# A graph-network kernel's setup in program order, with the first block's loads in two parts

## The chip, the cores and the metric

The kernel runs on one core of one Trainium2 chip. The metric is the device time of one execution in microseconds (us), the median of several runs. A core has five engines, each with an instruction queue of its own that is worked off in order: TensorE (PE, matrix products; its weight loads are shown as PEld), VectorE (DVE), ScalarE (ACT), GpSimd (POOL) and SyncE (SP, which here only issues DMAs and loads registers). An engine waits for another one, or for a DMA, on semaphores. A DMA is issued by an instruction of SP, ACT or POOL; it then runs on the core's 16 DMA engines and reports when its data has landed.

## What is computed

The kernel computes one layer of a graph network over 6250 nodes and 206250 edges, a residual sum and a layer norm. Cut to what matters here:

```
msg  = concat([x[dst], edge_attr])            # one row per edge, 64 + 64 wide
h    = relu(msg @ W1a.T + b1a)                # 128 wide
h    = h @ W1b.T + b1b
sums = segment_sum(h, src, 6250)              # rows of edges added at their source node
agg  = sums / max(counts, 1)
z    = relu(concat([x, agg]) @ W2a.T + b2a) @ W2b.T + b2b
x    = layernorm(x + concat([z, x]) @ Wr.T + br)
```

The edges are sorted by `dst`; `src` is in no order. So the gather of `x[dst]` is local, and the sum over `src` is what has to be brought together.

## The kernel before

The edges are cut into 1612 tiles of 128, and 13 tiles make a block: 124 blocks. Since the edges are sorted by `dst`, all the nodes that one block needs lie in a window of 60 nodes (`WIN`) that begins at a number, the window's start, of that block's own. For each block the kernel does the following.

- `group` (lines 1345 to 1370) loads what the block needs, on SP's queue. For the first eight blocks (`NEAR`) these are the target numbers of the block's 1664 edges, repeated over 60 partitions (`rhs<-in_dst_o`, L1352), the edges' features (`rhs<-in_edgeT`, L851), and the 60 node rows of the window (`rt<-in_xT`, L1356). The last load starts at the window's start, so SP first loads that number into a register out of `win_i` (L1355), a small table that DVE makes from the loaded `base_i` (L742).
- `columns` (L1386, DVE) compares the target numbers with the 60 nodes of the window, whose numbers stand in `near_f` (L986). The result is the upper half of the left operand `rhs` of the first layer.
- `window` (L1394, PE, and L1395, ACT) multiplies the window's node rows with the node half of W1a; ACT copies the result into `mv`, the other operand.
- `hidden` (L1427, PE, and L1431, ACT) is the first layer: one matmul of two passes per tile, and a relu by ACT into `orow`, three or four tiles at a time.
- `carried`, `bins_of`, `counts_of` and `slots` give each edge its place in a table of rows in DRAM, sorted by source node: DVE finds the edge's bin, the high bits of `src` (`hi`, L751 and L752, then L1092), and runs a scan over the block's tiles (L1098). PE makes counts of it with two triangular matrices, `less_ones` and `less_before` (L1140, L1141, into `cnt_ps`, of which there is one). DVE reduces them (L1238) and writes the row numbers `rowidx` (L1247).
- `scatter` (L1479, POOL) writes the 13 tiles of `orow` to the table, one indirect DMA per tile. From block 4 to block 109 six or nine tiles of a block are first sorted by PE in groups of four rows (`join`, `marks`, L1280 to L1343), and the scatter of a group (L1451) writes four rows at a time. So these blocks take nine or seven scatters in place of 13.
- Rows that are complete are read back (L1559, SP), and PE adds them up per node with one-hot matrices (L1593 on DVE, L1613 on PE). At the end of the kernel the node layers and the layer norm follow.

The order on PE, ACT, DVE and SP in the loop over the blocks is the order in which the program is written. Before the loop (lines 686 to 1800) a scheduler sets the order. POOL's order is the scheduler's throughout. The loop begins with this prologue, in which the numbers are those of blocks:

```
for g in range(3):
    made[g] = group(g)
window(0)
carried(0)
counts = counts_of(0, *bins_of(0))
columns(0)
slots(0, counts)
```

After it, block 0's `hidden` runs in four parts of 4, 3, 3 and 3 tiles; then come `window(1)`, `columns(1)`, `carried(1)` and `bins_of(1)`, and so on. In what is set up before the loop, `part_f` is each partition's own number, `in_win` (L941) and `from_win` (L939) are made from it, and `ramp` (L937) is the row 0 to 127. `one_w`, `before_w`, `four_w`, `more_w`, `less_w`, `of_quads`, `bases` and `even` are used by the joins from block 4 on; `ones` by the loads of node rows and by ACT from later blocks on; `bad` and `out_of` by checks.

Of the kernel before, what the change touches and what calls it, by code (L numbers as in the profile page):

```python
# [18 lines left out]
P = 128  # L19
# [459 lines left out]
NODES = 8  # L479

# [8 lines left out]
def fast_path(  # L489
# [69 lines left out]
    def direct(k):  # L559
        return BLK - JOIN * joined(k)  # L560
# [124 lines left out]

    base_i = const.tile([1, NGR], I32, name="base_i")
    nc.sync.dma_start(base_i, first.rearrange("(o g) -> o g", o=1))
# [8 lines left out]
    nc.sync.dma_start(src_i[:, :HEAD], srcT[:, :HEAD])  # L696
    near_i = const.tile([P, NEAR], I32, name="near_i")
# [18 lines left out]
    nc.vector.memset(mvs, 0.0)  # L716
# [12 lines left out]
    nc.vector.tensor_scalar(eye_b, diff_i, 0.0, BIG, op0=ALU.is_equal, op1=ALU.mult)  # L729
    ones = const.tile([P, P], F32, name="ones")  # L730
    nc.vector.memset(ones, 1.0)
# [3 lines left out]
    nc.vector.tensor_copy(part_f, part_i)  # L735
    nc.gpsimd.memset(near[: D + 1], 1.0)
    for e, ep_ in enumerate(epochs):
        ep_.tot = const.tile([P, 2 * HALF], F32, name=f"tot{e}")
# [3 lines left out]
    nc.vector.tensor_scalar(win_i, base_i, float(N - WIN), None, op0=ALU.min)  # L742
# [6 lines left out]
    def bins(c0, c1):  # L749
        tmp_i = lent(NT, NT)[:, c0:c1].bitcast(I32)  # L750
        nc.vector.tensor_scalar(tmp_i, src_i[:, c0:c1], 7, None, op0=ALU.arith_shift_right)  # L751
        nc.vector.tensor_copy(hi[:, c0:c1], tmp_i)  # L752
        nc.vector.tensor_scalar(tmp_i, src_i[:, c0:c1], P - 1, None, op0=ALU.bitwise_and)
        nc.scalar.copy(lo[:, c0:c1], tmp_i)

    ident = const.tile([P, P], F32, name="ident")
    make_identity(nc, ident)
    nc.vector.tensor_copy(mvs[:, :, H:], ident[:, None, WIDE : WIDE + 2].to_broadcast([P, MV, 2]))
# [6 lines left out]
    with (  # L765
# [83 lines left out]
        def edges(g):  # L849
            n = direct(g)  # L850
            nc.sync.dma_start(rhss[g % EDGES][:D, : n * P], edgeT[:, ((g + 1) * NG - n) * P : (g + 1) * NG * P])  # L851
# [9 lines left out]
        nc.vector.memset(out_of, 0.0)  # L861
# [77 lines left out]
        nc.vector.tensor_scalar(from_win, part_f, -1.0, float(D), op0=ALU.mult, op1=ALU.add)  # L939
        in_win = steady[:, RAMP : RAMP + 1]  # L940
        nc.vector.tensor_scalar(in_win, part_f, float(-D), None, op0=ALU.add)  # L941
# [5 lines left out]
        def starts_at(joints):  # L947
# [11 lines left out]
        one_w = const.tile([P, P], BF16, name="one_w")  # L959
        nc.vector.memset(one_w, 1.0)  # L960
        before_w = const.tile([P, P], BF16, name="before_w")
        nc.vector.scalar_tensor_tensor(
            before_w, diff_i, 0.0, eye_b, op0=ALU.is_gt, op1=ALU.add
        )
        less_ones = const.tile([P, P], BF16, name="less_ones")
        nc.vector.memset(less_ones, -1.0)
        less_before = const.tile([P, P], BF16, name="less_before")
# [3 lines left out]
        bins(0, HEAD)  # L971
# [12 lines left out]
        for g, i in ((2, NQB * 2), (3, NQB * 4)):  # L984
            assert NQB * (BLK - JOIN * g + 1) + i <= 512 and NQB * JOIN * g + NQB * 3 * (3 - g) <= 512
        nc.vector.tensor_scalar(  # L986
            near_f[D:WIDE, :], near_i[D:WIDE, :], float(N - WIN), in_win[D:WIDE, :], op0=ALU.min, op1=ALU.add
        )

        def row_of(value, name):  # L990


            w = const.tile([P, P], BF16, name=name)
            nc.vector.memset(w, 0.0)
            nc.vector.memset(w[:1, :], value)
            return w

        four_w, more_w, less_w = row_of(float(QUAD), "four_w"), row_of(1.0, "more_w"), row_of(-1.0, "less_w")
# [3 lines left out]
        for c, b in zip(of_quads, bases):  # L1002
            nc.vector.memset(c, FULLQUADS)
            nc.vector.memset(c[:, :, NQB:], FULLQUADS + P)
            nc.vector.memset(b, 0.0)
# [3 lines left out]
        nc.vector.memset(even_1, FULLQUADS)  # L1009
        even = even_1.to_broadcast([P, NQB])  # L1010
# [1180 lines left out]
```

## Time and profile before

| | |
|---|---|
| median of three runs | 1558.59 us |
| the three runs | 1558.59, 1557.15 and 5025.22 us |
| the profiled execution | 1557.99 us |
| its span, first to last instruction | 1556.1 us |
| mean granted TensorE clock | 0.978 |

The profile is of one execution. A row of its timeline gives the start and the length in us, the engine (SPq and ACTq are the instructions with which SP and ACT issue a DMA), the line of the program, the operation, what is written from what, the size (partitions x elements) and how many instructions are taken together; in brackets stands the time that the engine was idle before, and what ended it. A table by stages gives, for stretches of the span, how long each engine was busy and how many instructions it ran, the granted clock, the share of time in which the DMA engines were busy, and what they moved per second. Groups of instructions are listed by line with their busy time, the mean of one in ns, and the idle time in front of them.

### The profile page before, as it was taken

How to read it: one execution, taken by the hardware profiler on the slowest of the kernel's cores; microseconds unless marked ns; L12 is line 12 of the kernel's file. 1: busy time of each engine (PE TensorE's matmuls, PEld its weight loads, DVE VectorE, ACT ScalarE, POOL GpSimd, SP SyncE). 2: the span in 40 equal slices, each digit the busy share in tenths (PEclk: the TensorE clock that was granted, in tenths of full speed). 3: DMA queues.
4: the chain of work that ended last, by engine and by line, in shares of the span. 5: the costliest groups of instructions: out<-in, count | busy, mean ns of one | idle time of the engine just before them, and what ended most of it. 6: DMA issues, size and time to landing. Idle time of an engine off the chain costs nothing.

```text
span 1556.1 us, 33587 instructions
## 1 busy us (share of the span) xinstructions
PE 1438.4 (92%) x10958; PEld 1271.3 (82%) x10958; DVE 1334.3 (86%) x2819; ACT 1111.2 (71%) x2393; POOL 1149.6 (74%) x1232
## 2 busy tenths in 40 slices
PE   6689999968999999899999989999999999999996
PEld 5567777757888888788887878889888899999885
DVE  7588988879888988889888989999999887877886
ACT  3289999878888888788878869887877743342014
POOL 5777777777777777777777777777777777777733
PEclk9699999999999999999999999999999999999998
DMA  8877888768887888687777667677687899999883
GB/s 211 232 234 269 284 271 269 254 221 254 268 255 226 266 263 259 195 258 229 228 248 217 219 216 230 218 230 239 207 264 237 254 325 332 347 317 305 276 243 97
DMA packets 248712, 387.82 MB, mean 249 GB/s; under 512 B 43285, under 2 KB 180311, under 8 KB 248527
## 3 DMA queue, kind: packets, MB, share of 16 engines
q1 hardware_dynamic: 167661, 220.81, 49.2%
q0 software_dynamic: 47904, 122.68, 22.2%
q10 hardware_dynamic: 32962, 42.08, 8.0%
q8 instruction: 89, 1.46, 0.4%
q14 instruction: 96, 0.79, 0.2%
HBM read 214.09 MB, written 171.32 MB: 248 GB/s over the span
## 4 chain that ended last, share of the span: by engine, by line
PE 52%; DMA 16%; ACT 13%; DVE 9%; issue 6%; POOL 3%; ACTq 1%; SPq 0%; DVEq 0%; POOLq 0%
PE place L1613 20%; PE place L1325 9%; DMA rows<-orow,rowidx 8%; PE place L1427 8%; PE place L1340 8%; DMA rt<-rows 4%; ACT marks L1291 3%; DMA rows<-orow,qidx 3%; ACT marks L1295 2%; ACT rhs L1381 2%; POOL rows L1479 2%; ACT orow L1431 2%; DVE oh L1593 2%; ACT rj L1330 2%; DVE ramp L1191 1%
## 5 line engine op out<-in xcount | busy, mean ns | idle before, releaser
L1479 POOL DMA_INDIRECT rows<-orow,rowidx x922 | 899.8, 976 | 289.8 <-issue 148.7
L1613 PE MATMUL place<-rt,oh 128*128 128x129 f32 x3952 | 483.9, 277 | 32.3 <-ACT orow L1343 18.2
L1613 PEld LDWEIGHTS place<-rt,oh 128*128 128x128 f32 x3952 | 466.6, 192 | 46.2 <-ACT orow L1343 19.7
L1593 DVE TENSOR_TENSOR oh<-ramp,rt 128x768 f32<-128x768 bf16 (+4 forms) x391 | 309.0, 823 | 35.5 <-DMA rt<-rows 34.2
L1431 ACT ACTIVATE orow<-place 128x512 f32<-128x512 f32 (+1 forms) x266 | 145.0, 545 | 186.5 <-PE place L1427 181.2
L1451 POOL DMA_INDIRECT rows<-orow,qidx x230 | 225.2, 979 | 70.1 <-issue 22.2
L1340 PE MATMUL place<-mv,rj 128*128 128x130 f32 x1840 | 243.1, 282 | 35.6 <-ACT rj L1330 30.2
L1280 DVE TENSOR_TENSOR marks<-quad_ramp,ramp 128x1024 fp32r<-128x1024 f32 x230 | 268.6, 1212 | 5.0 <-ACT z_act L1194 5.0
L1427 PE MATMUL place<-mv,rhs 124*128 124x128 f32 x1844 | 265.2, 289 | 5.5 <-ACT orow L1431 5.5
L1340 PEld LDWEIGHTS place<-mv,rj 128*128 128x128 f32 x1840 | 220.5, 192 | 51.0 <-ACT rj L1330 37.5
L1325 PE MATMUL place<-marks,side 128*128 128x512 f32 x690 | 261.3, 408 | 0.0
L1427 PEld LDWEIGHTS place<-mv,rhs 124*128 124x128 f32 x1844 | 232.8, 198 | 7.2 <-ACT orow L1431 5.7
L1325 PE MATMUL place<-marks,rest 128*64 128x512 f32 x690 | 234.6, 394 | 0.0
L1325 PEld LDWEIGHTS place<-marks,side 128*128 128x128 f32 x690 | 130.9, 190 | 50.2 <-issue 0.8
L1295 ACT ACTIVATE marks<-marks,ones 128x512 fp32r<-128x512 f32 x230 | 166.8, 725 | 4.1
L1291 ACT ACTIVATE marks<-quad_ramp,z_act 128x512 fp32r<-128x512 f32 x230 | 166.0, 722 | 3.4 <-PE place L1325 0.9
L1343 ACT ACTIVATE orow<-place 128x260 f32<-128x260 f32 x460 | 159.3, 390 | 9.8 <-PE place L1340 1.4
L1098 DVE TENSOR_TENSOR_SCAN had<-ramp,bins 128x400 bf16<-128x400 bf16 (+2 forms) x124 | 128.4, 1036 | 23.9 <-ACT orow L1418 11.3
L1330 ACT COPY rj<-place 128x512 f32<-128x512 f32 x230 | 131.2, 571 | 0.8 <-PE place L1325 0.8
L1381 ACT ACTIVATE rhs<-rhs,ones 60x896 f32<-60x896 f32 (+2 forms) x116 | 123.8, 1067 | 3.0
L1379 ACT ACTIVATE rhs<-rhs,from_win 60x896 f32<-60x896 bf16 (+2 forms) x116 | 123.6, 1065 | 2.6
L1325 PEld LDWEIGHTS place<-marks,rest 128*64 128x64 f32 x690 | 93.5, 136 | 37.7 <-issue 0.4
(194 smaller groups left out, 1586.9 us busy)
## 6 DMA issues: line engine op xcount, KB each, us to landing
rt<-rows SPq DMA_DIRECT2D x194, 390.0 KB
rt<-rows SPq DMA_DIRECT2D x97, 325.0 KB
rows<-padrow ACTq DMA_DIRECT2D x24, 1040.0 KB
rhs<-in_edgeT SPq DMA_DIRECT2D x88, 224.0 KB
enat<-in_edgeJ SPq DMA_DIRECT2D x88, 192.0 KB
rows<-orow,rowidx POOLq DMA_INDIRECT x922
rt<-rows SPq DMA_DIRECT2D x40, 260.0 KB
rt<-rows SPq DMA_DIRECT2D x48, 195.0 KB
```

What stands on the lines that cost most here:

```text
L1280: nc.vector.tensor_tensor(m[:, :n, :], all_q[:, None, :].to_broadcast([P, n, QUAD * P]), z[:, :n, None].to_broadcast([P, n, QUAD * P]), op ...
L1291: nc.scalar.activation(m[:, t, :], all_q, AF.Square, bias=z_acts[k][:, i * JOIN + t : i * JOIN + t + 1], scale=-1.0)
L1295: nc.scalar.activation(m[:, t, :], m[:, t, :], AF.Relu, bias=ones[:, :1], scale=-1.0)
L1325: done[k, f"turn{i}"] = nc.tensor.matmul(ps[: w.shape[1], :], w, m[:, t, :], start=t + p == 0, stop=last and p == 1).ins.name
L1330: nc.scalar.copy(rj, ps)
L1340: done[k, f"join{i}"] = nc.tensor.matmul(ps[:, j, :], rj[:, (g0 + j) * P : (g0 + j + 1) * P], m, start=True, stop=True).ins.name
L1427: done[k, c] = nc.tensor.matmul(ps[:, j, :], rhs[:WIDE, of * P : (of + 1) * P], m[:WIDE, :H], start=True, stop=True).ins.name
L1431: nc.scalar.activation(orow_of(k, k0, n)[:, :, :H], ps[:, :n, :], AF.Relu)
L1451: s = nc.gpsimd.indirect_dma_start(out=qep.rows.rearrange("(q r) f -> q (r f)", r=QUAD), out_offset=bass.IndirectOffsetOnAxis(ap=qidx[:, q ...
L1479: s = nc.gpsimd.indirect_dma_start(out=ep_.rows, out_offset=bass.IndirectOffsetOnAxis(ap=rowidx[:, k % RING * BLK + j : k % RING * BLK + j ...
L1593: nc.vector.tensor_tensor(res[:, at_tile : at_tile + nb * n, :], ramp[:, None, :].to_broadcast([P, nb * n, P]), node[:, :, None].to_broadc ...
L1613: m = nc.tensor.matmul(of_bin(b), oh[:, at, :], rows, start=i == 0, stop=i == len(of) - 1)
```

## The change

The change touches what runs before the loop and in block 0.

- The setup on PE, ACT, DVE and SP is now in the order in which it is written, as the loop was already.
- On DVE the constants that the first counts need come first, then `win_i`, the bins of the first blocks and the scan. `later_consts` holds the other constants: 19 instructions that stood ahead of block 0's work and now stand behind it, in front of `columns(1)`.
- `base_i` is loaded from ACT's queue, ahead of ACT's three other loads, and no longer as the first load of SP. `part_f` is copied by ACT and not by DVE. The zeroes of `mv` are written by POOL, to the lower 64 partitions only, and so are its last two columns.
- Block 0's target numbers and edge features come in two parts: the first four tiles (`FIRST`) ahead of the window's rows, the other nine behind them. `columns(0)` is cut in the same way, and its second part stands behind `slots(0)`. `bins` is cut into high bits and low bits, and the low bits of the first blocks come later.
- Block 0's `hidden` runs in five parts, of 1, 3, 3, 3 and 3 tiles.

```diff
+FIRST = 4
...
+    in_order = ctx.enter_context(ExitStack())
+    in_order.enter_context(
+        tc.manual_schedule(
...
     base_i = const.tile([1, NGR], I32, name="base_i")
-    nc.sync.dma_start(base_i, first.rearrange("(o g) -> o g", o=1))
...
     nc.sync.dma_start(src_i[:, :HEAD], srcT[:, :HEAD])
+    nc.scalar.dma_start(base_i, first.rearrange("(o g) -> o g", o=1))
...
-    nc.vector.memset(mvs, 0.0)
...
-    nc.vector.tensor_copy(part_f, part_i)
+    nc.scalar.copy(part_f, part_i)
...
-    def bins(c0, c1):
+    def high_bins(c0, c1):
         tmp_i = lent(NT, NT)[:, c0:c1].bitcast(I32)
         nc.vector.tensor_scalar(tmp_i, src_i[:, c0:c1], 7, None, op0=ALU.arith_shift_right)
         nc.vector.tensor_copy(hi[:, c0:c1], tmp_i)
+
+    def low_bins(c0, c1):
+        tmp_i = lent(NT, NT)[:, c0:c1].bitcast(I32)
         nc.vector.tensor_scalar(tmp_i, src_i[:, c0:c1], P - 1, None, op0=ALU.bitwise_and)
         nc.scalar.copy(lo[:, c0:c1], tmp_i)
...
+    nc.gpsimd.memset(mvs[D:], 0.0)
     make_identity(nc, ident)
-    nc.vector.tensor_copy(mvs[:, :, H:], ident[:, None, WIDE : WIDE + 2].to_broadcast([P, MV, 2]))
+    nc.gpsimd.tensor_copy(mvs[:, :, H:], ident[:, None, WIDE : WIDE + 2].to_broadcast([P, MV, 2]))
...
-        bins(0, HEAD)
+        nc.vector.tensor_scalar(in_win, part_f, float(-D), None, op0=ALU.add)
+        one_w = const.tile([P, P], BF16, name="one_w")
+        before_w = const.tile([P, P], BF16, name="before_w")
+        nc.vector.tensor_scalar(win_i, base_i, float(N - WIN), None, op0=ALU.min)
+        high_bins(0, HEAD)
...
+        def first_places():
+            nc.vector.tensor_scalar(
+                near_f[D:WIDE, :], near_i[D:WIDE, :], float(N - WIN), in_win[D:WIDE, :], op0=ALU.min, op1=ALU.add
+            )
+
+        def later_consts():
+
+            nc.vector.memset(ones, 1.0)
+            nc.vector.tensor_scalar(from_win, part_f, -1.0, float(D), op0=ALU.mult, op1=ALU.add)
+            nc.vector.memset(out_of, 0.0)
+            nc.vector.memset(bad, 0.0)
+            nc.vector.memset(one_w, 1.0)
+            nc.vector.scalar_tensor_tensor(
+                before_w, diff_i, 0.0, eye_b, op0=ALU.is_gt, op1=ALU.add
+            )
+            for w, value in ((four_w, float(QUAD)), (more_w, 1.0), (less_w, -1.0)):
+                nc.vector.memset(w, 0.0)
+                nc.vector.memset(w[:1, :], value)
+            for c, b in zip(of_quads, bases):
+                nc.vector.memset(c, FULLQUADS)
+                nc.vector.memset(c[:, :, NQB:], FULLQUADS + P)
+                nc.vector.memset(b, 0.0)
+            nc.vector.memset(even_1, FULLQUADS)
...
-                s = nc.sync.dma_start(rhs[D:WIDE, :].bitcast(I32), all_of.to_broadcast([WIN, n * P]))
-                edges(g)
+                first_of = slice(0, FIRST * P if g == 0 else n * P)
...
+                s = part_of(first_of)
                 with tc.issue_after(s.ins):
                     w = nc.sync.value_load(win_i[0:1, g : g + 1], min_val=0, max_val=N - WIN)
                 nc.sync.dma_start(near[:D, g, :], xT[:, bass.ds(w, WIN)])
+                if g == 0:
+                    part_of(slice(FIRST * P, n * P))
...
-        columns(0)
+        first_places()
+        columns(0, of=slice(0, FIRST * P))
+        low_bins(0, HEAD)
         slots(0, counts)
+        columns(0, of=slice(FIRST * P, BLK * P))
...
-                hidden(k, ((0, 4), (4, 3), (7, 3), (10, 3)))
+                hidden(k, ((0, 1), (1, 3), (4, 3), (7, 3), (10, 3)))
+                later_consts()
                 window(1)
```

How the instructions stand before and after, with what each waits for (a DMAHW is a DMA's semaphore; the number behind a tile's name is only an identifier). The line numbers of after are its own: L1374 is L1352 of before, L865 is L851, L1382 is L1355, L1383 is L1356, L1257 is L1238, L1266 is L1247 and L1416 is L1386.

First place, ACT's queue at its start. Before:

```order
L712 DMA w1x_t<-in_W1a 64x128
L713 DMA w1x_t<-in_b1a 1x128
L717 DMA mv<-in_W1a 64x5x128 [waits DVE_49]
L754 ACT_TABLE_LOAD
L754 CAST lo<-rt 128x117 [waits DVE_49]
```

Now:

```order
L706 DMA base_i<-in_first 1x124
L722 DMA w1x_t<-in_W1a 64x128
L723 DMA w1x_t<-in_b1a 1x128
L726 DMA mv<-in_W1a 64x5x128
L741 ACT_TABLE_LOAD
L741 CAST part_f<-part_i 128x1 [waits Pool_49]
```

The load of `base_i` has come in front, and the copy of `part_f` stands behind ACT's loading of its function table. The same place on DVE, where `win_i` is made. Before:

```order
L994 MEMSET less_w 128x64
L742 TENSOR_SCALAR win_i<-base_i 1x124 [waits DMAHW1_49]
L995 MEMSET less_w 1x128 [waits DVE_49]
L1003 MEMSET of_quads_215 128x153
L751 TENSOR_SCALAR rt<-rt 128x117 [waits DMAHW3_49]
L1004 MEMSET of_quads_215 128x3 [waits DVE_49]
```

Now:

```order
L977 TENSOR_TENSOR less_before<-less_before,rt 128x128 [waits DVE_49]
L979 TENSOR_SCALAR ramp<-part_f 128x1 [waits Activation_49]
L982 TENSOR_SCALAR win_i<-base_i 1x124 [waits DMAHW0_49]
L757 TENSOR_SCALAR rt<-rt 128x117 [waits DMAHW1_49]
L758 CAST hi<-rt 128x117 [waits DVE_49]
L1132 MEMSET bins 128x50
L1111 TENSOR_TENSOR bins<-ramp,hi 128x50x13 [waits DVE_49]
L1117 SCALAR_TENSOR_TENSOR had<-ramp,bins 128x700 [waits DVE_49]
```

`win_i` now stands right behind `in_win` (L979, a column of the tile `ramp`), which waits for ACT's `part_f`, and the bins and the scan of block 0 stand behind both.

Second place, SP's queue at its start. Before:

```order
L687 DMA base_i<-in_first 1x124
L696 DMA rt<-in_srcT 128x117
L698 DMA near_i<-in_first 60x8
L1352 DMA rhs_148<-in_dst_o 60x1664
L851 DMA rhs_148<-in_edgeT 64x1664
L1355 TENSOR_LOAD win_i
L1355 ISA x2
L1356 REGISTER_ALU
L1356 DMA rt<-in_xT 64x60
L1352 DMA rhs_149<-in_dst_o 60x1664
```

Now:

```order
L705 DMA rt<-in_srcT 128x117
L708 DMA near_i<-in_first 60x8
L1374 DMA rhs_147<-in_dst_o 60x512
L865 DMA rhs_147<-in_edgeT 64x512
L1382 TENSOR_LOAD win_i
L1382 ISA x2
L1383 REGISTER_ALU
L1383 DMA rt<-in_xT 64x60
L1374 DMA rhs_147<-in_dst_o 60x1152
L865 DMA rhs_147<-in_edgeT 64x1152
L1374 DMA rhs_148<-in_dst_o 60x1664
```

Ahead of block 0's window rows (`rt<-in_xT`) stand 512 of the 1664 columns; the other 1152 stand behind them and in front of block 1's loads.

Third place, DVE behind block 0's counts. Before:

```order
L1238 TENSOR_REDUCE row<-cnt_ps 128x13 [waits PE_49]
L1247 SCALAR_TENSOR_TENSOR rowidx<-row,bin_at 128x13 [waits DVE_49]
L1386 TENSOR_TENSOR rhs_149<-rhs_149,ramp 60x1664 [waits DMAHW1_49]
L1115 TENSOR_TENSOR bins<-had,ramp 128x50
L1092 TENSOR_TENSOR bins<-ramp,hi 128x50x13
```

Now, up to the ninth of the 19 instructions of `later_consts` (the others are of the same kinds, and `columns(1)` follows them):

```order
L1257 TENSOR_REDUCE row<-cnt_ps 128x13 [waits PE_49]
L1266 SCALAR_TENSOR_TENSOR rowidx<-row,bin_at 128x13 [waits DVE_49]
L1416 TENSOR_TENSOR rhs_147<-rhs_147,ramp 60x1152 [waits DMAHW1_49]
L1014 MEMSET ones 128x128
L1015 TENSOR_SCALAR from_win<-part_f 128x1
L1016 MEMSET out_of 128x2
L1017 MEMSET bad 128x50
L1018 MEMSET one_w 128x128
L1019 SCALAR_TENSOR_TENSOR before_w<-rt 128x128
L1023 MEMSET four_w 128x64
L1024 MEMSET four_w 1x128 [waits DVE_49]
L1023 MEMSET more_w 128x64
```

Between block 0's row numbers and `columns(1)` there was nothing; now the second part of `columns(0)` and `later_consts` stand there.

More of the change, by code (lines that the diff above doesn't have):

```diff
@@ L683, in fast_path @@
     ep = by_edge.enter_context(tc.tile_pool(name="fedge", bufs=1))
+    in_order = ctx.enter_context(ExitStack())
+    in_order.enter_context(
+        tc.manual_schedule(
+            engines={
+                mybir.EngineType.PE, mybir.EngineType.Activation, mybir.EngineType.DVE, mybir.EngineType.SP
+            }
+        )
+    )
     base_i = const.tile([1, NGR], I32, name="base_i")
-    nc.sync.dma_start(base_i, first.rearrange("(o g) -> o g", o=1))
     rt_all = ep.tile([P, READS, RD * W], F32, name="rt")
@@ L958, in fast_path @@
         starts_at(0)
[L959 to L964, printed above, removed]
         less_ones = const.tile([P, P], BF16, name="less_ones")
         nc.vector.memset(less_ones, -1.0)
+        nc.vector.tensor_scalar(eye_b, diff_i, 0.0, BIG, op0=ALU.is_equal, op1=ALU.mult)
         less_before = const.tile([P, P], BF16, name="less_before")
@@ L985, in fast_path @@
             assert NQB * (BLK - JOIN * g + 1) + i <= 512 and NQB * JOIN * g + NQB * 3 * (3 - g) <= 512
[L986 to L998, printed above, removed]
+        four_w, more_w, less_w = (const.tile([P, P], BF16, name=n) for n in ("four_w", "more_w", "less_w"))
         FULLQUADS = 128.0
@@ L1351, in group, with part_of @@
                 all_of = dst[((g + 1) * NG - n) * P : (g + 1) * NG * P].rearrange("(o e) -> o e", o=1)
-                s = nc.sync.dma_start(rhs[D:WIDE, :].bitcast(I32), all_of.to_broadcast([WIN, n * P]))
-                edges(g)
+                first_of = slice(0, FIRST * P if g == 0 else n * P)
+                def part_of(of):
+                    s = nc.sync.dma_start(
+                        rhs[D:WIDE, of].bitcast(I32), all_of[:, of].to_broadcast([WIN, of.stop - of.start])
+                    )
+                    edges(g, of)
+                    return s
+                s = part_of(first_of)
                 with tc.issue_after(s.ins):
@@ L1370, in group, with columns @@
             return rhs, rel, m
-        def columns(g, part_of=0):
+        def columns(g, part_of=0, of=None):
             rhs, rel, _ = made[g]
@@ L1385, in columns @@
             if part_of == 0:
+                of = of or slice(0, direct(g) * P)
                 nc.vector.tensor_tensor(
-                    rhs[D:WIDE, :], rhs[D:WIDE, :].bitcast(I32),
-                    near_f[D:WIDE, g : g + 1].to_broadcast([WIN, direct(g) * P]), op=ALU.is_equal,
+                    rhs[D:WIDE, of], rhs[D:WIDE, of].bitcast(I32),
+                    near_f[D:WIDE, g : g + 1].to_broadcast([WIN, of.stop - of.start]), op=ALU.is_equal,
                 )
```

33 lines of the change are left out of this document (10 added, 23 removed).

## The prediction

> **What bounds the kernel now.** I read the page first, for who is busy. Its first part and the two costliest groups of POOL:
>
> ```profile
> PE 1438.4 (92%) x10958; PEld 1271.3 (82%) x10958; DVE 1334.3 (86%) x2819; ACT 1111.2 (71%) x2393; POOL 1149.6 (74%) x1232
> L1479 POOL DMA_INDIRECT rows<-orow,rowidx x922 | 899.8, 976 | 289.8 <-issue 148.7
> L1451 POOL DMA_INDIRECT rows<-orow,qidx x230 | 225.2, 979 | 70.1 <-issue 22.2
> ```
>
> By shares PE would be the bound. But POOL's 1152 scatters have 359.9 us of idle time in front of them, about 0.31 each, which looks like a fixed gap. So I read POOL's timeline, the stretch between its first and last scatter, and the semaphore instructions at the joins' scatters:
>
> ```profile
> 13.71 1.15 POOL L1479 DMA_INDIRECT rows<-orow,rowidx  x1 [9.07 <-ACT orow L1431]
> ...
> 30.43 0.97 POOL L1479 DMA_INDIRECT rows<-orow,rowidx  x1 [0.30 <-issue]
> ...
> 46.98 0.97 POOL L1479 DMA_INDIRECT rows<-orow,rowidx  x1 [0.30 <-ACT orow L1431]
> ...
> 1488.58 0.97 POOL L1479 DMA_INDIRECT rows<-orow,rowidx  x1 [0.30 <-issue]
> 13.71:1488.58 1474.87, 1381.88 (x10551) 1221.87 (x10551) 1273.78 (x2627) 1085.63 (x2256) 1124.02 (x1151) 0.98 0.81 255
> L1451 POOLq EVENT_SEMAPHORE  x230: 17/17/43, 84.8 to 1250.4; - x115
> ```
>
> The reader is to see one unbroken row of scatters: 1151 of them in 1474.87 us, 1.28 us from start to start, 0.97 busy and 0.30 gap. The 350.8 us of gaps behind the first scatter (359.9 less 9.07) are 0.305 each, and no semaphore at a join's scatter held POOL for more than 43 ns. So POOL waits once, for its first scatter. What comes behind the last one hangs on it too, by the rows of the end (SP's waits from 1440 to 1500 us, then DVE and PE):
>
> ```profile
> SPq L1559 <- DMA rows<-orow,rowidx: 5.8, 3, 4.6
> 1461.74 1.42 DVE L1593 TENSOR_TENSOR oh<-ramp,rt 128x768 f32<-128x768 bf16 x2 [1.45 <-DMA rt<-rows]
> 1462.75 22.97 PEld L1613 LDWEIGHTS place<-rt,oh 128*128 128x128 f32 x202 [2.13 <-DVE oh L1593]
> ```
>
> SP's reads wait for scatters, DVE for the reads, PE for DVE. So the time is the start of the first scatter, plus the row of scatters, plus a tail that moves with it. A change in the first 14 us is worth what it moves the row, if no later scatter then has to wait.
>
> **The chain to the first scatter.** The timeline of the first 14 us:
>
> ```profile
> 0.76 0.34 SPq L687 DMA_DIRECT2D base_i<-in_first  x1
> 1.15 0.37 SPq L696 DMA_DIRECT2D rt<-in_srcT  x1
> 2.46 0.50 DVE L742 TENSOR_SCALAR win_i<-base_i 1x124 int32<-1x124 int32 x1
> 2.58 0.56 SPq L851 DMA_DIRECT2D rhs<-in_edgeT  x1
> 2.79 1.28 ACT L754 ACT_TABLE_LOAD   x1 [2.79 <-DVE less_w L994]
> 3.22 0.22 DVE L751 TENSOR_SCALAR rt<-rt 128x117 int32<-128x117 int32 x1 [0.17 <-DMA rt<-in_srcT]
> 4.08 0.29 ACT L754 CAST lo<-rt 128x117 bf16<-128x117 int32 x1
> 4.51 0.51 SPq L1356 DMA_DIRECT2D rt<-in_xT  x1
> 7.07 1.61 DVE L1098 TENSOR_TENSOR_SCAN had<-ramp,bins 128x700 bf16<-128x700 bf16 x1
> 9.14 0.65 PE L1394 MATMUL place<-w1x_t,rt 65*60 65x128 f32 x2 [9.14 <-DMA rt<-in_xT]
> 10.87 5.12 PE L1427 MATMUL place<-mv,rhs 124*128 124x128 f32 x26
> 11.98 0.17 DVE L1247 SCALAR_TENSOR_TENSOR rowidx<-row,bin_at 128x13 int32<-128x13 f32 x1
> 12.19 1.89 DVE L1386 TENSOR_TENSOR rhs<-rhs,ramp 60x1664 f32<-60x1664 int32 x1
> 12.82 0.60 ACT L1431 ACTIVATE orow<-place 128x512 f32<-128x512 f32 x1 [2.49 <-PE place L1427]
> ```
>
> The window's rows are issued at 4.51 and PE starts on them at 9.14, 4.63 us later, since they queue behind 0.8 MB of block 0's loads. Behind the window PE makes the counts, then four tiles of the first layer; ACT is done at 13.42 and POOL starts 0.29 later. The row numbers were ready at 12.15.
>
> **The change, part by part, up to the first scatter.**
>
> `win_i` comes later. ACT issues one DMA more, for `base_i`: 0.39 us by SP's own spacing of it (0.76 to 1.15); ACT's two spacings could make it 0.7. Its table load then ends at 2.79 + 0.39 + 1.28 = 4.46, and `part_f` some 0.17 later, priced by a small copy of ACT:
>
> ```profile
> 55.72 0.17 ACT L1194 COPY z_act<-ramp 128x6 f32<-128x6 f32 x1 [1.32 <-DVE ramp L1191]
> 0.96 0.60 DVE L716 MEMSET mv<- 128x650 f32 x1 [0.96 <-PEq L2173]
> 0.96:6.20 5.24, 4.91 (x38) 1.00 0.72 168
> 12.19:22.36 10.17, 9.97 (x9) 0.98 1.03 229
> ```
>
> `win_i` starts about 4.76 and ends 5.26, where it ended at 2.96: 2.30 later. Behind the waiting `in_win` all of DVE's block 0 is queued: shift, cast, bins and scan, done about 8.15 by their durations, and the four tiles of `columns(0)` (1.89 x 512/1664 = 0.58) at 9.0. Before PE needs them, so this wait of DVE costs only by way of `win_i`.
>
> SP waits for `win_i` with everything else behind it. It issued the window's rows 1.55 us after `win_i`, so now at 6.81. What stands ahead in the DMA engines is 0.5 MB (58 KB sources, 120 and 128 KB of block 0's first part, 192 KB from ACT), all issued by about 3.2; at the 168 GB/s of the stretch from 0.96 to 6.20 that is 3 us, done near 6. So they should land on idle engines. The price of that is between the 2.07 us of `srcT` (1.15 to DVE's start at 3.22), with almost nothing ahead, and the 4.63 of now. I take 2.07, since the queue is then nearer to that row. PE's window starts at 8.88, 0.26 earlier than before, though the load was issued 2.3 later.
>
> From there to the row numbers nothing changes: they are ready at 12.15 - 0.26 = 11.89. The rows are no longer last: with `columns` done, PE runs the first tile right behind the counts at about 10.6, one of four that took 12.82 - 10.87 = 1.95 together, and ACT's relu of 128 columns is at most 0.60: done by 11.8. The first scatter starts at 11.89 + 0.29 = 12.18, **1.53 us earlier**.
>
> **Block 1 takes half of it back.** DVE has two new pieces ahead of `columns(1)`: the rest of `columns(0)`, 1.89 x 1152/1664 = 1.31, and the 19 instructions of `later_consts`. The 38 setup instructions from 0.96 to 6.20 (above) took 0.138 us each; without the two largest (0.58 for `mv`, 0.33 for `win_i`, to the next start) and the wait of 0.17, 36 took 0.116. 19 of them are 2.2 us, at most 2.6. They stood ahead of block 0, hidden behind its loads; now DVE's work for block 1 hangs on them. It was busy 9.97 of the 10.17 us from 12.19 to block 1's counts, so nothing absorbs it. `columns(1)` moves by 1.31 + 2.2 - 0.26 = 3.25 us. The chain behind, DVE's reduce that frees `cnt_ps`, PE's counts and first layer, ACT's rows:
>
> ```profile
> 21.55 0.81 DVE L1238 TENSOR_REDUCE row<-cnt_ps 128x13 f32<-128x650 f32 x1
> 23.53 3.29 PE L1427 MATMUL place<-mv,rhs 124*128 124x128 f32 x20
> 25.48 1.21 ACT L1431 ACTIVATE orow<-place 128x512 f32<-128x512 f32 x2 [6.99 <-PE place L1427]
> ...
> 32.26 1.16 ACT L1431 ACTIVATE orow<-place 128x512 f32<-128x512 f32 x2 [0.57 <-PE place L1427]
> ```
>
> The first relu of block 1 ended at 25.48 + 0.60 = 26.08, 4.4 us before its scatter at 30.43. Now it ends at 29.33, and the scatter can start at 29.62. POOL would be there at 12.18 + 16.72 = 28.90 and waits 0.72. What is left at block 1 is 30.43 - 29.62 = **0.81 us**.
>
> Block 2 has slack for 3.25: its first rows were ready at 32.26 + 0.6, its scatter came at 46.98. And from 40 to 80 us PE stood still for 14.5 of 40 us, which takes in its delay:
>
> ```profile
> 40.00:60.00 20.00, 11.07 (x57) 9.74 (x55) 12.77 (x25) 6.89 (x16) 15.13 (x17) 0.65 0.84 231
> 60.00:80.00 20.00, 14.42 (x75) 11.32 (x74) 9.96 (x28) 5.57 (x15) 15.36 (x16) 0.67 0.71 213
> ```
>
> Costed at nothing: POOL's extra memset and copy (`mv`, about 0.6 by DVE's row above), since POOL is idle until its first scatter; one more relu of ACT, since ACT waits for PE in blocks 0 and 1. SP's two extra issues and its wait move block 1's loads by about 3.5 us: block 0's rest and block 1's target numbers are 0.95 MB from 7.4 on, 4.2 us at the 229 GB/s above, so landed near 13, two us before `columns(1)` at 15.4. Without that cover each us late is one more at block 1.
>
> The sum: the profiled execution, 1557.99, would take 1557.18; it lies 0.60 under the median of the runs, 1558.59, which becomes 1557.8.
>
> [...] ACT's `lo` starts at 4.08, 0.01 after the table load's end. [...]
>
> **Rivals.**
>
> - *Slower: the window's rows land as late as now.* If they take 4.63 us from their new issue at 6.81, PE's window starts at 11.44, the first scatter at 14.7, and block 1's at 30.43 + 2.30 + 1.31 + 2.2 - 4.35 (the 30.43 - 26.08 of slack) + 0.29 = 32.18: 1.75 later, 1560.3. For it: `win_i` is 2.3 later in any case, and ACT's 160 KB for `mv` share the engines. Against it: the engines should be empty by then. It decides from a landing of 2.07 + 0.81 = 2.9 us on.
> - *All of the 1.53 is kept*, 1557.1: DVE is through with `later_consts` in under 1.5 us, since small memsets overlap. Against it stands 0.116 each.
> - *The lead is lost later*, 1558.6: scatters also wait for PE's progress by written-in dependencies, and PE is busy 1381.88 of 1474.87 us. Then the row starts earlier and stops somewhere. Against it: no wait over 43 ns at the joins' scatters now; for it: how near to waiting they are, the trace does not show.
> [...]
>
> **How the numbers follow.** Forecast 0.50, slower by the landing 0.18, lead lost 0.14, all kept 0.11, a hold behind the table load 0.04, something without a price 0.03. Two per cent are 31 us, about what a measurement of this kernel can tell from no change, and all the priced cases lie within 2 us: within 2% 0.97, faster 0.01, slower 0.02. The range goes from the best case less the spread of the two close runs (1557.1 - 1.4 = 1555.7) to the landing case with 0.34 more for ACT's issue (1560.7).
>
> **What would show it.** POOL's first scatter near 12.2; `win_i` at 4.8 and the window's rows issued near 6.8, PE starting on them near 8.9; a gap of about 1 us before block 1's first scatter, which starts near 29.6, and none behind it; the last scatter near 1487.8. I am wrong if PE's window starts after 9.8, if block 1's scatter comes after 30.4, or if POOL shows new gaps after 40 us.

## The result, and the profile after

| | before | after |
|---|---|---|
| median | 1557.5 us (6 runs, one of them 5025.22 us) | 1543.83 us (6 runs, 1542.21 to 1546.22) |
| ratio | | 0.9923, 95% interval 0.9912 to 0.9933 |
| span of the profiled execution | 1556.1 us | 1540.4 us |
| first scatter starts | 13.71 us | 12.76 us |
| last scatter starts | 1488.58 us | 1476.03 us |
| from there to the end | 67.5 us | 64.4 us |

The kernel became 13.7 us faster by the medians. The 0.8 us that were forecast at the start are not what made it: 0.43 us of the earlier start were left at block 1, and the gain lies elsewhere. The spans differ by 15.7 us: the row of scatters starts 0.95 earlier, is 11.60 shorter (1474.87 against 1463.27) and has a tail that is 3.15 shorter.

The page of the kernel after, its first part and POOL's two groups of scatters (`scatter` is now at L1509 and L1481):

```profile
PE 1431.7 (93%) x10958; PEld 1266.1 (82%) x10958; DVE 1334.6 (87%) x2817; ACT 1110.7 (72%) x2395; POOL 1136.8 (74%) x1234
L1509 POOL DMA_INDIRECT rows<-orow,rowidx x922 | 890.2, 966 | 289.9 <-issue 134.8
L1481 POOL DMA_INDIRECT rows<-orow,qidx x230 | 221.1, 961 | 70.1 <-issue 20.4
```

The counts are the old ones. The idle time in front of the scatters is the old one too (289.9 and 70.1); but the wait for the first scatter fell in it from 9.07 to 7.18 us, so the gaps behind it rose from 350.8 to 352.8. What fell is the busy time, from 1125.0 to 1111.3 us over the same 1152 scatters, 976.6 to 964.7 ns each on average. These 13.7 us less the 2.0 us of new gaps are the shorter row. The views of these two lines give the duration as minimum, median and maximum in ns, of before and of after:

```profile
L1479 POOL DMA_INDIRECT rows<-orow,rowidx x922: 963/968/1759, 13.7 to 1488.6; - x185
...
L1451 POOL DMA_INDIRECT rows<-orow,qidx x230: 966/970/1433, 92.5 to 1254.3; - x115
```

```profile
L1509 POOL DMA_INDIRECT rows<-orow,rowidx x922: 954/958/1429, 12.8 to 1476.0; - x185
...
L1481 POOL DMA_INDIRECT rows<-orow,qidx x230: 956/960/1227, 92.3 to 1243.7; - x115
```

The reader is to see that the minimum and the median moved together, by 9 to 10 ns. So it is not that fewer scatters were disturbed: the undisturbed ones are shorter, too. The median is 958 ns in each eighth of the row of after and 968 to 970 in each of before. From start to start it is 1271.3 ns on average in place of 1281.4.

The timeline of the start and of block 1, for the steps of the prediction:

```profile
3.08 1.28 ACT L741 ACT_TABLE_LOAD   x1 [3.08 <-issue]
4.37 0.19 ACT L741 CAST part_f<-part_i 128x1 f32<-128x1 int32 x1
4.59 0.99 POOL L1070 MEMSET room<- 128x7 f32 x26
4.67 0.98 DVE L982 TENSOR_SCALAR win_i<-base_i 1x124 int32<-1x124 int32 x1
6.75 0.50 SPq L1383 DMA_DIRECT2D rt<-in_xT  x1
8.87 0.65 PE L1424 MATMUL place<-w1x_t,rt 65*60 65x128 f32 x2 [8.87 <-DMA rt<-in_xT]
11.71 0.18 DVE L1266 SCALAR_TENSOR_TENSOR rowidx<-row,bin_at 128x13 int32<-128x13 f32 x1
11.91 1.36 DVE L1416 TENSOR_TENSOR rhs<-rhs,ramp 60x1152 f32<-60x1152 int32 x1
12.76 1.18 POOL L1509 DMA_INDIRECT rows<-orow,rowidx  x1 [7.18 <-DVE rowidx L1266]
13.36 0.17 DVE L1014 MEMSET ones<- 128x128 f32 x1
15.83 1.89 DVE L1416 TENSOR_TENSOR rhs<-rhs,ramp 60x1664 f32<-60x1664 int32 x1
...
29.13 0.60 ACT L1461 ACTIVATE orow<-place 128x512 f32<-128x512 f32 x1 [6.17 <-PE place L1457]
30.00 0.96 POOL L1509 DMA_INDIRECT rows<-orow,rowidx  x1 [0.92 <-ACT orow L1461]
...
77.63 0.96 POOL L1509 DMA_INDIRECT rows<-orow,rowidx  x1 [0.84 <-DMA rows<-orow,rowidx]
...
85.95 0.97 POOL L1509 DMA_INDIRECT rows<-orow,rowidx  x1 [1.05 <-ACT marks L1310]
```

PE's window starts at 8.87 and the row numbers are ready at 11.89, as forecast. Block 1's first scatter waits for its rows and comes at 30.00, 0.43 before its old time. Two more waits follow, at 77.63 and 85.95, of 0.84 and 1.05 us where 0.30 is usual. At 142 us POOL is 0.1 us ahead of its old times (a scatter at 142.48 that stood at 142.56); from there on the lead grows by 11.9 ns a scatter to 12.55 us, which is what the mean length fell by.

The tail: behind the last store of the output SP passes eight waits (L2188 before, L2214 after) and the end. Duration in ns, and the times of the first and the last of them; then, from a DMA view that begins 2.5 us behind the last store's issue, the loads of instructions (number, MB, share):

```profile
L2188 SPq EVENT_SEMAPHORE  x8: 17/17/17, 1551.7 to 1554.4; - x8
...
q14 instruction: 3, 0.02, 1.2%
```

```profile
L2214 SPq EVENT_SEMAPHORE  x8: 17/17/17, 1538.2 to 1538.7; - x8
...
q14 instruction: 2, 0.02, 1.9%
```

Eight instructions of 17 ns took 2.7 us before and 0.5 after, with three loads of instructions in that stretch before and two after. Before, two of the eight stand at 1551.7 to 1551.8 and six at 1554.0 to 1554.4, and one of the loads (8192 bytes, at 1552.5) lies in the break between them; after, none lies between the eight. From the issue of the last store to the end it is 8.6 us before (1547.53 to 1556.1) and 5.5 after (1534.93 to 1540.4), which is all of the tail's 3.1 us.

### The profile page after: what moved, and what is told of

The parts are those of the page before. It is cut to its first block, busy times and chain, and to the rows that moved or that the text cites. A ratio compares the mean times of both kernels' runs of the same rounds, so it can differ in the third digit from the quotient of the medians.

```text
span 1540.4 us, 33598 instructions
## 1 busy us (share of the span) xinstructions
PE 1431.7 (93%) x10958; PEld 1266.1 (82%) x10958; DVE 1334.6 (87%) x2817; ACT 1110.7 (72%) x2395; POOL 1136.8 (74%) x1234
## 4 chain that ended last, share of the span: by engine, by line
PE 55%; DMA 16%; ACT 12%; DVE 6%; issue 5%; POOL 2%; SPq 2%; ACTq 1%; DVEq 0%; POOLq 0%
PE place L1643 21%; PE place L1344 10%; PE place L1359 8%; PE place L1457 8%; DMA rows<-orow,rowidx 8%; DMA rt<-rows 4%; ACT marks L1310 3%; DMA rows<-orow,qidx 2%; ACT marks L1314 2%; ACT rhs L1410 2%; ACT rj L1349 2%; POOL rows L1509 2%; ACT orow L1461 2%; DVE oh L1623 1%; DVE marks L1299 1%
## 5 line engine op out<-in xcount | busy, mean ns | idle before, releaser
L1509 POOL DMA_INDIRECT rows<-orow,rowidx x922 | 890.2, 966 | 289.9 <-issue 134.8
L1461 ACT ACTIVATE orow<-place 128x384 f32<-128x384 f32 (+2 forms) x267 | 145.0, 544 | 185.1 <-PE place L1457 172.4
L1481 POOL DMA_INDIRECT rows<-orow,qidx x230 | 221.1, 961 | 70.1 <-issue 20.4
```

The source lines that it names most:

```text
L1461: nc.scalar.activation(orow_of(k, k0, n)[:, :, :H], ps[:, :n, :], AF.Relu)
L1481: s = nc.gpsimd.indirect_dma_start(out=qep.rows.rearrange("(q r) f -> q (r f)", r=QUAD), out_offset=bass.IndirectOffsetOnAxis(ap=qidx[:, q ...
L1509: s = nc.gpsimd.indirect_dma_start(out=ep_.rows, out_offset=bass.IndirectOffsetOnAxis(ap=rowidx[:, k % RING * BLK + j : k % RING * BLK + j ...
```

## The experiments

Two questions: what shortens the scatters, and what shortens the end? From block 1 on the order of the instructions is the same on every engine. Ahead of that the order differs on four engines, and POOL has a memset and a copy more, both for `mv`. The addresses of `rowidx`, `qidx`, `orow` and the table are the same in both programs. Theory A: POOL's own two instructions do it. Theory B: the order of the setup on the other engines does. Theory C: it depends on where the program is loaded.

**Each part by itself.** `e1` is before plus POOL's two pieces, `e2` is after without them, `e3` is before with two more memsets on POOL, `e4` is before with the setup in program order.

```diff
 e1: before
-    nc.vector.memset(mvs, 0.0)
...
+    nc.gpsimd.memset(mvs[D:], 0.0)
     make_identity(nc, ident)
-    nc.vector.tensor_copy(mvs[:, :, H:], ...)
+    nc.gpsimd.tensor_copy(mvs[:, :, H:], ...)
 e2: after, with these two pieces on DVE (the memset of `mvs[D:]` alone, ahead of the loads)
 e3: before
-    nc.gpsimd.memset(eps, EPS)
+    for _ in range(3):
+        nc.gpsimd.memset(eps, EPS)
 e4: before, with `in_order` entered ahead of `base_i`
```

> The kernel before, with only the two pieces of the change that add instructions to POOL: the zeroes of mv (lower 64 partitions) and its last two columns are written by POOL. Theory A (POOL's own two added instructions make each later scatter about 10 ns shorter): median busy time of a scatter near 966 ns, time near 1544.5 us. Theory B (it is the new order of the setup on the other four engines, or the numbering of the semaphores that follows from it): scatters stay at 976 ns, time 1557 us. Theory C (the scatters' length depends on where the loaded program happens to lie, not on what is in it): any value, and no pattern over the four kernels of this group.

> The changed kernel with only those two pieces undone: mv's zeroes and last columns are written by DVE again, first of its work, and POOL has as many instructions as before. Theory A: scatters back at 976 ns, time near 1557 us. Theory B: scatters stay at 966 ns, time 1544 to 1545 us (DVE's start is up to 1 us later). Theory C: any value.

> The kernel before with two more small memsets on POOL in the setup (the same value written to eps again), which shift POOL's instructions by two and do nothing else. Theory A in its form that only the count or place of POOL's instructions matters: 966 ns, 1544.5 us. Theory A in its form that the copy on POOL matters, and theory B: 976 ns, 1557.5 us. Theory C: any value.

> The kernel before with one edit: the order of the setup on PE, ACT, DVE and SP is that of the program (the manual order begins ahead of the setup); no instruction is added, removed or moved to another engine. Theory B: scatters at 966 ns, time near 1544 to 1546 us. Theory A: 976 ns, about 1557 us, with the first scatter at another time than 13.71. Theory C: any value.

Measured: e1 1548.56 us, ratio 0.9943 (0.9927 to 0.9960). e2 1554.40, 0.9988 (0.9978 to 0.9997). e3 1555.96, 0.9996 (0.9986 to 1.0006). e4 1558.97, 1.0016 (1.0006 to 1.0026). The scatters' line in e1, and in e2:

```profile
L1479 POOL DMA_INDIRECT rows<-orow,rowidx x922: 952/958/1708, 14.2 to 1474.8; - x185
```

```profile
L1509 POOL DMA_INDIRECT rows<-orow,rowidx x922: 963/967/1383, 12.0 to 1483.0; - x185
```

POOL's two pieces carry the short scatters with them, into the old kernel and out of the new one. In e3 and e4 the median is 967. Theory A stands in the form that it is the copy, the memset or both. All the rest of the change together (e2) is worth 0.5 to 3.4 us. e1 gained 4 us less than was expected of it; where they went is said below.

**The copy or the memset, and where.** `e5` has one copy of one column in the setup, `e6` only the memset of `mv`. `e7` has the copy in the middle of the row, and `e8` five small instructions between the scatters.

```diff
 e5: before
     nc.gpsimd.memset(eps, EPS)
+    nc.gpsimd.tensor_copy(eps, eps)
 e6: before, the memset alone of the two pieces of e1
 e7: before, ahead of nothing that needs it
             if k >= LEAD:
                 scatter(k - LEAD)
+            if k == 60:
+                nc.gpsimd.tensor_copy(part_i.bitcast(F32), orow_of(k - 1, BLK - 1)[:, 0, :1])
 e8: the same place, at k = 20, 40, 60, 80, 100:
     tensor_scalar, tensor_tensor, tensor_copy, tensor_tensor, tensor_scalar
```

> The kernel before with one instruction more: a copy of one column (eps onto itself) on POOL in the setup. Theory A1 (the copy, as a kind of instruction that POOL had not run before its scatters, makes them shorter): median near 958 ns in place of 968, row of scatters 10 to 11 us shorter, time 1545 to 1549 us. Theory A2 (the large memset of mv on POOL does it): 968 ns and no change, 1556 us. Theory A3 (both are needed, or it is DVE's relief from them): no change either.

> The kernel before with only the zeroes of mv moved from DVE to POOL; the copy of its last two columns stays on DVE. Theory A1: median of a scatter stays 968 ns, 1556 us. Theory A2: 958 ns, 1545 to 1549 us. Theory A3: no change.

> The kernel before with one small copy (one column of block 59's rows into the unused part_i) on POOL in the middle of the row of scatters, near 720 us. Theory A1 with an effect that lasts: median 968 ns for the scatters ahead of the copy and 958 for those behind it, with the step at the copy; last scatter 5 us earlier than 1488.6. If only instructions in the setup count, or the place of POOL's instructions in memory: one value from the first to the last scatter.

> The kernel before with five small instructions of one column on POOL between its scatters: a product with a constant (tensor_scalar) at block 20, a sum of two operands (tensor_tensor) at block 40, a copy at block 60, tensor_tensor again at 80 and tensor_scalar again at 100. Theory A1 (each kind leaves POOL in a state of its own): steps in the median length of a scatter at some of the five, 958 ns behind the copy at least from 60 to 80. If only the first of any such instruction matters: one step, at block 20, and none later. If the copy alone matters: 968 ns up to block 60 and 958 behind it.

Measured: e5 1546.37 us, 0.9934 (0.9918 to 0.9951), median 958 ns. e6 1557.07, 1.0006 (0.9996 to 1.0015), 968 ns. The scatters' line in e5, and in e6:

```profile
L1480 POOL DMA_INDIRECT rows<-orow,rowidx x922: 954/958/1330, 14.7 to 1474.8; - x185
```

```profile
L1479 POOL DMA_INDIRECT rows<-orow,rowidx x922: 963/968/1665, 13.7 to 1486.9; - x185
```

So one copy of 128 numbers, which nobody needs, gives 10 us, and the memset gives nothing. e7 (1556.21 in one run) went the other way from what was expected: 967 ns ahead of its copy and 969 behind it. e8 (1556.24 in one run) showed why that is no contradiction. Its scatters at L1479, stretch by stretch between the five instructions:

```profile
L1479 POOL DMA_INDIRECT rows<-orow,rowidx x142: 952/959/1706, 14.6 to 239.7; - x142
...
L1479 POOL DMA_INDIRECT rows<-orow,rowidx x125: 963/968/1249, 241.1 to 457.0; - x125
...
L1479 POOL DMA_INDIRECT rows<-orow,rowidx x132: 965/970/1391, 458.4 to 681.7; - x132
...
L1479 POOL DMA_INDIRECT rows<-orow,rowidx x132: 965/970/1298, 684.3 to 905.9; - x132
...
L1479 POOL DMA_INDIRECT rows<-orow,rowidx x131: 954/959/1336, 907.3 to 1127.2; - x131
...
L1479 POOL DMA_INDIRECT rows<-orow,rowidx x258: 963/967/1278, 1130.0 to 1485.3; - x129
```

The median length of a scatter is constant between two computing instructions of POOL and can change at them: 959, 968, 970, 970, 959, 967. The kind does not say which value follows: the same `tensor_tensor` left 970 once and 959 once. I had also expected 968 up to block 20, since the setup on POOL is that of before, and it was 959. That was the moment to give up "a copy makes scatters short" for theory S: what POOL computed last leaves the scatters behind it at one of a few lengths. Theory S does not account for e8's first stretch either: ahead of it POOL computes what it computes in the kernel before, where the scatters take 968 ns.

**Is it settled by the program?** `e9` has the copy as POOL's last instruction ahead of the first scatter, `e10` a `tensor_scalar` in place of e5's copy. `e11` is e8 again, and `e12` is the changed kernel with a `tensor_scalar` near block 20.

```diff
 e9: before, behind the memsets of `room`
+        last_room = epochs[-1].room[:, NB - 1 : NB]
+        nc.gpsimd.tensor_copy(last_room, last_room)
 e10: before
     nc.gpsimd.memset(eps, EPS)
+    nc.gpsimd.tensor_scalar(eps, eps, 1.0, None, op0=ALU.mult)
 e12: after, behind scatter(k - LEAD)
+            if k == 20:
+                nc.gpsimd.tensor_scalar(part_i.bitcast(F32), orow_of(k - 1, BLK - 1)[:, 0, :1], 2.0, None, op0=ALU.mult)
```

> The kernel before with one copy of one column on POOL as its last instruction ahead of the first scatter (in the small-copy kernel 30 memsets followed the copy). Theory K (a copy in the setup makes the scatters short): median 958 ns, 1545 to 1548 us. Theory S (whatever POOL computes last ahead of the row leaves the row's length in one of a few values, and the kind does not say which): 958 or 967 ns, time 1546 or 1556 us with it.

> The kernel before with one product of one column (eps times 1.0) on POOL in the setup, at the place where the small-copy kernel has its copy. Theory K: median stays 968 ns, 1556 us, since it is no copy. Theory S: 958 or 967, and time with it. If one more instruction of any kind but memset does it: 958 ns, 1546 us.

> The same kernel as that with five small instructions, once more: does each stretch keep its value? If the value is settled by the program: 959, 968, 970, 970, 959 and 967 ns again. If it is settled anew in each execution: other values, and ahead of the first of the five 968 ns as in the kernel before, whose setup on POOL is the same.

> The changed kernel with one product of one column on POOL between two scatters near block 20 (some 240 us), where the five-instruction kernel went from 959 to 968 ns. Theory S: 958 ns ahead of it, and a step there, to 967 or 968 in the likeliest case; the row then loses some 980 x 0.010 = 9.5 us of its gain, and the time is near 1553 us. Theory K: 958 ns throughout and 1544 to 1545 us, since one instruction of 0.25 us is all that is added.

These four ran on a chip on which the kernel before takes 1993.97 us (25 runs, 1980.22 to 2006.74). e9: 1993.58, ratio 0.9989 (0.9955 to 1.0023). e10: 1992.92, 0.9992 (0.9974 to 1.0010). e11: 2001.54 in one run. e12: 1988.18, 0.9964 (0.9932 to 0.9997). POOL's group of scatters in e9:

```profile
L1481 POOL DMA_INDIRECT rows<-orow,rowidx x922 | 890.1, 965 | 650.6 <-issue 199.8 <-ACT orow L1433 106.4 <-PE place L1327 89.8
```

The scatters are short here too (median 962), but POOL stood idle in front of them for 650.6 us in place of 290, and ACT and PE account for much of that: POOL waits for others all along the row there, and no gain from shorter scatters shows. One of up to 9 us in e9 and of some 5 us in e10 lies within the intervals. Why that chip is slower was not looked into. What the group did settle is the length. e11 gave 958, 967, 969, 969, 958, 967 ns, e8's sequence within 1 ns on another chip, with every wait at another time. So the program settles the sequence, not the execution, and theory C falls as far as the place of a program changes from one loading to the next. e9 and e10 had 962 throughout, so a `tensor_scalar` does in the setup what the copy does; e12 went from 962 to 971 at its added instruction. These values lie 4 ns above those of the same programs on a faster chip (e16 and e15, next: 958, and 958 to 967); why, the runs do not show.

**The time with it, and what is left.** e12 and e10 were repeated beside the changed kernel itself (`e14`). `e13` is e2 with e5's small copy: the start without POOL's pieces, and the short scatters.

> The changed kernel with mv's two pieces back on DVE, and one copy of one column on POOL in the setup in their place. Theory S, with what the runs so far show: the setup's part (first scatter near 12.0 as in the kernel with mv on DVE, since win_i is not held) and the short scatters (958 ns) add up: time 1542 to 1544.5 us where the kernel before takes 1556 to 1557, the same as the changed kernel or up to 1 us below it. If the copy holds DVE up as it held the cast in the small-copy kernel (1.27 us in place of 0.27): first scatter near 13, and no better than the changed kernel. If the length is not set by the copy here: 967 ns, 1554 us.

> The changed kernel itself, in one group with the others: 958 ns and 1543 to 1545 us if the length of a scatter is settled by the program; 967 ns and 1554 us in some of the runs if it is settled by the execution.

> The changed kernel with one product of one column on POOL near block 20, once more: 958 ns ahead of it and 967 to 968 behind it, so 975 x 0.0095 = 9 us given back, 1552 to 1554 us (theory S). If what the profile shows as the length of a scatter does not count for the time: 1544 us, as the changed kernel.

> The kernel before with one product of one column on POOL in the setup, once more: 958 ns and 1546 to 1548 us, as with the small copy (theory S: any such instruction can do it); 968 ns and 1556 us if only a copy does.

Measured: e13 1549.36 us, 0.9946 (0.9932 to 0.9960). e14 1544.39, 0.9917 (0.9903 to 0.9931). e15 1554.32, 0.9983 (0.9971 to 0.9994). e16 1549.49, 0.9956 (0.9940 to 0.9972), 958 ns. e15's scatters ahead of and behind its one added instruction of 0.27 us:

```profile
L1509 POOL DMA_INDIRECT rows<-orow,rowidx x142: 954/958/1562, 12.7 to 239.4; - x142
...
L1509 POOL DMA_INDIRECT rows<-orow,rowidx x779: 962/967/1527, 242.1 to 1486.7; - x195
```

That instruction costs the changed kernel 9.9 us (1554.32 against 1544.39), as 975 scatters of some 10 ns more should; in the profiles the row is 10.6 us longer. e13 was a miss: its scatters have 958 ns and start at 12.47, yet it is 5 us slower than e14. Its eight waits of SP at the end run from 1541.5 to 1544.1, broken as before. In the built programs SP's stream has one instruction more than before in e1, e2 and e13, and two more in the changed kernel, in e14 and in e15; of these only the last three have the unbroken end. The break is some 2 us of e13's 5.

The profiles show most of the rest, and of what e1 lacked, behind the last scatter. From its start to POOL's first instruction of the node layers (`agg`) it is 14.82 us in the kernel before, 14.77 and 14.85 in the two profiles of the changed kernel, but 16.58 in e13, 17.21 in e15 and 21.06 in e1. So e13's span is 4.6 us above e14's, 1.7 by this and 2.3 by the end; and e1's row is 14.3 us shorter than before's, while its span is only 7.8 shorter, since 6.2 went here. What sets this stretch the runs do not show.

**The end.** `e17` gives SP two more loads in the old kernel, so that it has as many instructions as in the changed one. `e18` has those and e5's copy: three instructions, and nothing of the change.

```diff
 e17: before
+            if k == 1:
+                nc.sync.dma_start(base_i, first.rearrange("(o g) -> o g", o=1))
+                nc.sync.dma_start(near_i[D:WIDE, :], first[:NEAR].rearrange("(o g) -> o g", o=1).to_broadcast([WIN, NEAR]))
 e18: e17, and
     nc.gpsimd.memset(eps, EPS)
+    nc.gpsimd.tensor_copy(eps, eps)
```

> The kernel before with two more small loads on SP in block 1 (base_i and near_i once more, which nobody reads again), so that SP has as many instructions as in the changed kernel. If the place of SP's last instructions against the boundary of an 8 KB load of instructions makes the end shorter: no break between SP's last waits, from the last store's issue to the end 5.5 to 6 us in place of 8.6, one load less behind the last store (8 in place of 9), time 2.0 to 3 us below the kernel before (1553.5 to 1555); scatters at 968 ns. If the shorter end comes from something else in the change: the break stays, time as the kernel before.

> The kernel before with those two loads on SP and the small copy on POOL in the setup, three instructions in all, and nothing of the change itself. If scatters and end explain the gain: 958 ns, no break at the end, time 1543.5 to 1545.5, as the changed kernel. If the change's own start is worth 1 us or more on top: 1545.5 to 1547.

Measured: e17 1554.50 us, 0.9988 (0.9979 to 0.9997). e18 1542.16, 0.9916 (0.9904 to 0.9929). SP's eight waits in e17, and then e18's waits and scatters:

```profile
L2190 SPq EVENT_SEMAPHORE  x8: 17/17/17, 1551.2 to 1551.8; - x8
```

```profile
L2191 SPq EVENT_SEMAPHORE  x8: 17/17/17, 1538.0 to 1538.5; - x8
...
L1480 POOL DMA_INDIRECT rows<-orow,rowidx x922: 954/958/1417, 14.7 to 1473.9; - x185
```

Two more instructions of SP's alone remove the break and 0.5 to 3.3 us. With the copy, three instructions without any use reproduce the whole gain: e18 cannot be told from the changed kernel (0.9923 and 0.9917 in its two groups), though its first scatter starts at 14.7, almost 2 us later. The row of all profiles on the faster chips says the same: 1470.4 to 1474.9 us in the seven with long scatters throughout (the kernel before has the longest), 1459.2 to 1464.0 in the seven with short ones.

## Why the prediction was wrong

**The step that failed** is the one that cost nothing in it: "Costed at nothing: POOL's extra memset and copy (`mv`, about 0.6 by DVE's row above), since POOL is idle until its first scatter." POOL had the time for them, but with them `win_i` took 0.98 us in place of e2's 0.20, and the first scatter came at 12.76 in place of 11.96. Above all the copy changed the length of the 1152 scatters behind it, and with them the term that the sum took as fixed, the row of "1.28 us from start to start". In its place the runs showed a median 9 to 10 ns lower, 11.6 us in the row. e1 and e5 put it in, e2 takes it out, e15 gives it back in the middle. That the copy does it is shown; by what mechanism stays open.

**The tail** was the second: "a tail that moves with it". It became 3.1 us shorter: two more instructions of SP's removed the break in its last waits, and e17 shows the same with two loads and nothing else.

Point by point for the rest:

- The chain to `win_i`: `part_f` at 4.37 (4.46 forecast), `win_i` from 4.67, but it took 0.98 and not 0.50. The window's rows were issued at 6.75 (6.81) all the same, since SP issued them 1.10 us behind the end of `win_i` and not 1.55 as before. Two errors cancelled, so the agreement from here to the row numbers is in part luck.
- The landing: 2.12 us (2.07 taken), and PE's window at 8.87 (8.88). The slower rival is out. So is a hold behind the table load, which the forecast gave 0.04: the load ran from 3.08 for 1.28 us, and `part_f` starts 0.01 behind its end.
- Row numbers at 11.89, as forecast. The first scatter came 0.87 behind them, where 0.29 was taken from a scatter that had waited for ACT: 12.76 in place of 12.18. This term was mis-sized.
- Block 1: the rest of `columns(0)` took 1.36 (1.31), `later_consts` 2.47 (2.2, at most 2.6), the first relu ended at 29.73 (29.33), the scatter came at 30.00 (29.62), and 0.43 of lead was left in place of 0.81.
- "None behind it": wrong. The two waits at 77.63 and 85.95 cost 0.54 and 0.75 us over the usual 0.30, more than the lead of 0.43. This is the rival of the lost lead. It does not come in every execution: in e14, which is the same program, neither wait is there, and at 142 us POOL is 1.17 us ahead of the profile of before.

So the part that was worked out was right in kind and, up to block 1, within 0.6 us. That a change of the start is worth what it moves the row is not shown to the microsecond: it fits e2 (first scatter 1.75 earlier, 0.5 to 3.4 us faster) and e4 (1.90 later, 0.9 to 4.0 slower), but e18 starts 1.96 later than the changed kernel and takes no longer. The two terms that the sum took as constant, the row and the tail, moved by 14.8 us together, where the first scatter moved by 0.95.

## What to carry to other kernels

Where one engine works off a thousand equal instructions without a break, their length is the first thing to compare between two profiles, minimum and median, before any wait is looked for: 10 ns there (11.6 us in the row) outweighed all the rest of the change (e2, 0.5 to 3.4 us). One instruction more on that engine was not "free" here, since the scatters behind it changed (e5's copy gave 10 us, e15's `tensor_scalar` took 9.9), so a change that adds one should be split from the rest and timed alone. And the gain belonged to its program: one later instruction undid most of it (e15), and on the chip of 1994 us it did not show (e9 0.9989, e10 0.9992).

## What the runs showed of the hardware

**A scatter of POOL has a few lengths.** Medians of 958 to 959 and 967 to 970 ns were seen on the chips on which the kernel before takes some 1556 us, constant between POOL's computing instructions and changed by some of them (`tensor_copy`, `tensor_scalar` and `tensor_tensor`; memsets alone did not change it in e3, 967, and e6, 968). e8's sequence came again on the slower chip within 1 ns, while the other three programs there have 962 and 971. All eight programs with a copy or a `tensor_scalar` in the setup have the shorter length; of those without, only e8 has it. The number of POOL's instructions does not decide it: in the built programs it is the same in e5 and e6 (958 and 968 ns), and in e1 and e3 (958 and 967). The mechanism stays open: no run here looks into POOL.

**Beside POOL's memsets an instruction of DVE took longer where the scatters are short.** In the setup POOL has a train of 26 memsets (`room`), which start 31 to 46 ns apart and take 1 us together. A cast of DVE (`hi`) meets it. The rows are of the kernel before, then of e5 and of e8:

```profile
3.48 0.27 DVE L752 CAST hi<-rt 128x117 bf16<-128x117 int32 x1
...
3.56 1.07 POOL L1051 MEMSET room<- 128x7 f32 x26
```

```profile
3.48 1.27 DVE L752 CAST hi<-rt 128x117 bf16<-128x117 int32 x1
...
3.69 0.98 POOL L1052 MEMSET room<- 128x7 f32 x26
```

```profile
3.41 1.22 DVE L752 CAST hi<-rt 128x117 bf16<-128x117 int32 x1
...
3.55 1.00 POOL L1051 MEMSET room<- 128x7 f32 x26
```

The same cast takes 0.27 us beside the train in the first; in the other two it takes 1.27 and 1.22 and ends 0.07 to 0.08 us behind the train's end. The profiles divide in this way without exception. In all twelve in which short scatters follow the train (the two of the changed kernel, e1, e5, e8, e10 to e13, e15, e16 and e18) a cast or `tensor_scalar` of DVE takes 0.71 (e13) to 1.42 us (e16) there. In six of the seven with long ones (the kernel before, e2, e3, e6, e7 and e17) those of more than one column take 0.20 to 0.36; in the seventh, e4, none runs inside the train. e9's copy stands behind the train, and its scatters are short (962 ns). So e8 was in that condition from its start, without a copy ahead of the train: whether from the execution before it or by what else its program holds, no run shows.

The same shows at `win_i` in the changed kernel: it ran from 4.67 to 5.65, and POOL's memsets to 5.58. In e2, which has no copy on POOL and was through with them before `win_i`, it took 0.20:

```profile
4.66 0.20 DVE L982 TENSOR_SCALAR win_i<-base_i 1x124 int32<-1x124 int32 x1
```

What lengthens DVE's instruction no run shows: in the kernel before the same cast takes 0.27 us beside the same train.

**SP's last waits can be broken**, at some 2 us for the break (2.7 us in place of 0.5 for eight waits of 17 ns), and in the kernel before a load of instructions (8192 bytes, at 1552.5) lies in the break. Two instructions more in SP's stream removed it, in the setup (the change) and in block 1 (e17); none or one more did not. All 20 profiles divide so: the waits take 0.5 to 0.6 us in the six with two more, and 2.4 to 2.9 us in the fourteen others. That it is the place of the waits against the boundaries of the loads fits this, and is not shown beyond it.
